# Two expert stages whose late tiles are opened before their last early tiles are done

## The chip, the cores and the metric

The kernel runs on one core of one Trainium2 chip. The metric is the device time of one execution in microseconds (us), the median of several runs. The core has a matrix engine (PE, with its weight loads PEld), a vector engine (DVE), a scalar engine (ACT), a general engine (POOL) and a sync engine (SP) that only issues transfers. Plain loads and stores are issued from SP. Gathers and scatters by an index list are issued from POOL.

## What is computed

The input has 2 sequences of 2048 tokens, 256 wide. Four layers follow, each on the layer-normed stream and added back to it: a state-space layer (Mamba-2), a mixture of experts, an attention layer over the two sequences, and the same mixture of experts again. Only the mixture matters here. It routes every token to 2 of 8 experts:

```python
scores = x @ Wr.T + br                      # 8 scores per token
idx    = top_k(scores + biases, 2)          # two experts for each token
val    = softmax(scores)[idx]; val /= val.sum()
h      = x @ Wl1[e] + bl1[e]                # 256 -> 2*512, for each expert e
y      = (silu(h[:512]) * h[512:]) @ Wl2[e] + bl2[e]      # 512 -> 256
out    = sum over the two experts of val * y
```

All of it is float32.

## The kernel before

**Tiles of tokens by expert.** Class `Experts` (L280) does one mixture; `ffn` (names ending in `_f`) is the first and `last` (names in `_g`) the second. Tokens are handled in 8 groups of 512. When a group is routed (`prepare`, L309), `enter` (L413) scatters an entry for each of its tokens and choices into a table in memory, eight scatters from POOL (L433), sorted by expert. A tile is 256 consecutive entries of one expert (128 for a half tile). For a tile the kernel does this:

- `rows` (L652): SP loads the tile's part of the table, `tab`.
- `load` (L663): SP loads the expert's first weights `w1` (1 MB), second weights `w2` (0.5 MB) and biases `b1`, `b2`.
- `gather` (L680): POOL gathers the tile's tokens from memory into `xs`, 128 at a time.
- `turn` (L702): PE transposes `xs` (4 transposes, L709) into a PSUM bank and ACT copies it out as `xT` (L713).
- `up` (L735): four times `up_part` (L716): PE multiplies `w1` into a bank (`pab`, L722), ACT takes the silu (L730), DVE multiplies into `gT` (L731).
- `down` (L743): PE multiplies `w2` (`pf`, L752), DVE adds the bias part (L765), POOL scatters the rows with addition (L776).

**Early and late tiles.** A tile that is sure to be full can run before all tokens are routed. These are the early tiles: 21 in the first mixture (called f-e0 to f-e20 here), mixed into the state-space layer, and 9 in the second (g-e0 to g-e8), mixed into the attention layer. The profile writes them `_fe` and `_ge`. The others are late tiles (f0, f1, ... and g0, g1, ...): 16 in the first mixture, 28 in the second, and they begin once `plan` (L516) knows every count. A seam is the place where the last early tile gives way to the first late one. Generator `early` (L788) is stepped by the layer around it; what is left of it runs in `tiles.rest()` (L1215 and L1476). Then `run` (L812) takes the late tiles in a loop, three tiles ahead with loads.

**Buffers.** There are two pools. `fe` exists throughout, with two buffers each of `w1`, `w2`, `b2`, `xs`, `y`. `f2` lies in memory that the layer before has given back, and opens with `run` (L817). Early tiles use `fe`; of the late tiles those with an odd place in the sequence use `fe`, those with an even place `f2` (L649). The first late tile has place 21 in the first mixture and 9 in the second, so in both it uses `fe` and its `w1` waits until the last early tile but one has been multiplied.

**Banks.** PSUM banks are handed out by tag, two banks for each of A, B, C and T. An early tile uses only tag B: for its transposes, all four up parts and the down part. A late tile transposes into T and alternates A and B.

**What sets the order.** SP's order is that of the program, by hand (L79). Every engine works its own list in order. Outside `run`, the order on PE, ACT, DVE and POOL comes from a planner that works when the program is built; inside `run` ACT, DVE and POOL stand in the order written (L818) and PE is left to the planner. In `early` a tile is turned, multiplied up and down, and then the next is turned. So in the second mixture SP's list has, one after another, the loads of g-e6, g-e7 and g-e8, then four `tab` loads, then the loads of g0 and g1.

Of the kernel before, what the change touches and what calls it, by code (L numbers as in the profile page):

```python
# [34 lines left out]
NT = NB * L  # L35
# [11 lines left out]
def kernel(  # L47
# [35 lines left out]
    def bank(tag, name):  # L83
        return ps.tile([P, 512], F32, tag=tag, name=name)
# [195 lines left out]
    class Experts:  # L280
        def __init__(self, name, acc, direct=False):
            self.name, self.acc, self.direct = name, acc, direct
            self.seq, self.ts, self.tabs, self.next = [], {}, {}, [0, 0, 0]
            n = NE * NT + TT
            self.table = tc.dram_tile([n + (NE * TT if direct else 0), 3], F32, name=f"table_{name}")
            self.xnd = tc.dram_tile([NT + TT, DM], F32, name=f"xnd_{name}")
            nc.sync.dma_start(self.table[:n, :].rearrange("(p r) c -> p r c", p=P), empty)
            for to in (self.xnd,) if direct else (self.xnd, acc):
                nc.sync.dma_start(to[NT:, :].rearrange("(h p) d -> p h d", p=P), zero)
            self.off = rt2.tile([P, NE], F32, tag=f"off{name}", name=f"off0_{name}")  # L290
            nc.gpsimd.tensor_copy(self.off, region)

            self.pay = const.tile([P, NT // P, 2, 3], F32, name=f"pay_{name}")
            for c, of in ((0, token), (2, place.rearrange("p s b t -> p (s b t)"))):
                nc.gpsimd.tensor_copy(
                    self.pay[:, :, :, c].bitcast(I32), of.unsqueeze(2).to_broadcast([P, NT // P, 2])
                )
            self.rest, self.freed = None, []
            if direct:
                self.rest = const.tile([P, TT // P, 3], F32, name=f"rest_{name}")  # L300
                nc.gpsimd.memset(self.rest, 0.0)
                for c, base in ((0, NT), (2, 0)):
                    nc.gpsimd.iota(
                        self.rest[:, :, c].bitcast(I32), [[P, TT // P]], base=base, channel_multiplier=1
                    )
            self.taken = rt2.tile([P, NE], F32, tag=f"taken{name}", name=f"taken_{name}")
            nc.gpsimd.memset(self.taken, 0.0)
# [208 lines left out]
        def plan(self):  # L516

            name = self.name
            NPT = 2 * NT // TT - len(self.seq)
            NTT = NPT + NHF  # L520
            cnt = rt1.tile([P, NE], F32, tag="cnt", name=f"cnt_{name}")
            nc.vector.tensor_tensor(cnt, self.off, region, ALU.subtract)
# [123 lines left out]

        def tile(self, i, shape, tag, dtype=F32, bufs=2):
            nm, _, _, _, early = self.seq[i]
            pool = fe if early or i % 2 else self.f2  # L649
            return pool.tile(shape, dtype, tag=tag, name=f"{tag}_{nm}", bufs=bufs)  # L650

        def rows(self, i):  # L652
# [38 lines left out]
        def fetch(self, tables, tiles, gather=True):  # L691
            while self.next[0] < min(tables, len(self.seq)):
                self.rows(self.next[0])
                self.next[0] += 1
            while self.next[1] < min(tiles, len(self.seq)):
                self.load(self.next[1])
                self.next[1] += 1
                if gather:
                    for h in range(2):
                        self.gather(self.next[1] - 1, h)  # L700

        def turn(self, i):  # L702
            t = self.ts[i]
            nm, nh = t["nm"], t["nh"]
            n = nh * P
            pt = bank("B" if self.seq[i][4] else "T", f"pxs_{nm}")
            for k in range(KD):
                for h in range(nh):
                    nc.tensor.transpose(  # L709
                        pt[:, k * n + h * P : k * n + (h + 1) * P], t["xs"][:, h, k * P : (k + 1) * P], ident  # L710
                    )
            xT = fe.tile([P, KD * TT], F32, tag="xT", name=f"xT_{nm}")
            nc.scalar.copy(xT[:, : KD * n], pt[:, : KD * n])  # L713
            t["xT"] = xT[:, : KD * n].rearrange("p (k t) -> p k t", k=KD)
# [20 lines left out]
        def up(self, i):  # L735
            t = self.ts[i]
            nm = t["nm"]
            pool = fe if i % 2 else self.f2
            t["gT"] = pool.tile([P, NHT, TT], F32, tag="gT", name=f"gT_{nm}", bufs=1)
            for j in range(NHT):  # L740
                self.up_part(t, j, "AB"[j % 2])
# [46 lines left out]
        def early(self, ready):  # L788

            i = 0  # L790
            while True:
                while i >= len(self.seq):
                    yield
                if not self.seq[i][4]:
                    return
                full = sum(t[4] > 0 for t in self.seq)
                self.fetch(min(i + 2, full), min(i + 2, full))
                self.fetch(full, 0)
                if not i:
                    yield  # L800
                self.turn(i)
                t = self.ts[i]
                t["gT"] = fe.tile([P, NHT, TT], F32, tag="gT", name=f"gT_{t['nm']}", bufs=1)
                for j in range(NHT):
                    self.up_part(t, j, "B")
                    if j % 2:
                        yield
                self.down(i, "B", None)
                i += 1
                yield  # L810

        def run(self):  # L812
            ahead = 3
            first = next(i for i, t in enumerate(self.seq) if not t[4])
            n = len(self.seq)
            with (
                tc.tile_pool(name=f"f2{self.name}", bufs=2) as self.f2,  # L817
                tc.manual_schedule(  # L818
                    engines={mybir.EngineType.Pool, mybir.EngineType.Activation, mybir.EngineType.DVE}
                ),  # L820
            ):
                self.fetch(first + ahead + 1, first + ahead)
                self.turn(first)
                assert self.seq[-1][1] == 2
                for i in range(first, n - 1):
                    self.fetch(i + ahead + 2, i + ahead + 1, gather=False)
                    if i == first + 6:
                        with tc.manual_schedule(engines={mybir.EngineType.PE}):
                            beyond = nc.values_load(self.beyond[0:1, 0:1], min_val=0, max_val=NHF - NIN)
                            self.up(i)  # L830
                    else:
                        self.up(i)
                    self.turn(i + 1)
                    if i > first:
                        self.down(i - 1, "C", i + ahead)
                    else:
                        for h in range(2):
                            self.gather(i + ahead, h)
                    if i == first + 2:
                        yield  # L840
                self.down(n - 2, "C", None)
                self.up(n - 1)
                self.down(n - 1, "C", None)
                with tc.If(beyond > 0):
                    for tile in self.more:
                        i = len(self.seq)
                        self.seq.append(tile)
                        self.fetch(i + 1, i + 1)
                        self.turn(i)
                        self.up(i)  # L850
                        self.down(i, "C", None)

    ffn = Experts("f", tc.dram_tile([NT + TT, DM], F32, name="resid"))
    last = Experts("g", flat(out), direct=True)
# [2 lines left out]
    with tc.tile_pool(name="ssm1", bufs=1) as s1, tc.tile_pool(name="ssm2", bufs=2) as s2:  # L857
# [339 lines left out]
            done = (b, s, t, y)  # L1197
        chunk_out(*done)
        aside.add(routing(*done[:2]))
        while aside.waiting:  # L1200
            aside.step()
            tiles.step()
# [9 lines left out]
    attw = ctx.enter_context(tc.tile_pool(name="attw", bufs=1))  # L1212
    w_qkv_sb = attw.tile([P, KD, 3, AW], F32, name="w_qkv_sb")
    w_o_sb = attw.tile([P, NA, DM], F32, name="w_o_sb")
    tiles.rest()  # L1215
    late = ffn.run()
    next(late)
# [8 lines left out]
    with tc.tile_pool(name="att1", bufs=1) as a1, tc.tile_pool(name="att2", bufs=2) as a2:  # L1226
# [230 lines left out]
        for s in range(NS):  # L1457

            if s + 1 < NS:
                while s + 1 not in inputs:  # L1460
                    aside.step()
                scores(s + 1, range(0, GT // 2))

                aside.waiting.insert(0, entered())
            else:
                aside.rest()
                tiles.step(4)
            mix(s)
            outward(s)
            if s + 1 < NS:  # L1470
                scores(s + 1, range(GT // 2, GT))
                weights(s + 1)
        while aside.waiting:
            aside.step()
            tiles.step()
        tiles.rest()  # L1476

    for _ in last.run():
        pass

# [60 lines left out]
```

## Time and profile before

| | us |
|---|---|
| runs: median, lowest, highest of 3 | 1701.59, 1696.14, 1702.38 |
| profiled execution, its own time | 1703.7 |
| span in that profile (first to last instruction) | 1702.0 |
| PE busy in the span | 1585.8 |
| first seam: last up of an early tile starts, first up of a late one starts | 729.42, 739.84 |
| second seam: the same | 1402.62, 1415.92 |
| late tiles of the second mixture, from there to PE's last matmul | 1415.92 to about 1691.7 |

The time of an execution is 1.7 us more than the span. Lines of the order in time have: start, duration, engine, line, operation, output and inputs, how often, and in brackets the idle time of the engine before it and what ended that. Consecutive instructions of a kind are merged, so a row's duration runs from its first start to its last end. Matmuls overlap a little, so the start of the next row is the better end. In the table of stretches every engine has its busy time and its instruction count, then come the granted clock of PE (1.00 is full), the busy share of the transfer engines and the rate in GB/s.

### The profile page before, as it was taken

The numbers are of one execution on the slowest core, as the hardware profiler recorded it, in microseconds if no ns is written. First come the engines' busy times: TensorE is split into PE (matmuls) and PEld (weight loads), VectorE is DVE, ScalarE is ACT, GpSimd is POOL, SyncE is SP. The second block draws the span as 40 slices with busy tenths as digits, with TensorE's granted clock in tenths as the row PEclk, the third lists the DMA queues.
The fourth block names the chain that finished last, engine by engine and source line by source line (L and its number), as shares of the span: only waits on it lengthen the run. The fifth ranks groups of instructions, "written<-read, shape, count | busy, mean of one in ns | idle before, by whom it ended". The sixth has DMA issues, their size and how long they took to land.

```text
span 1702.0 us, 22149 instructions
## 1 busy us (share of the span) xinstructions
PE 1585.8 (93%) x7088; PEld 1194.0 (70%) x7088; DVE 896.3 (53%) x2471; ACT 674.6 (40%) x1340; POOL 739.0 (43%) x702
## 2 busy tenths in 40 slices
PE   6997988989999989999998999899999979999997
PEld 3665555677767767788984575465768768888886
DVE  6778878837648464422227648447454512222222
ACT  5886867856647543222332202011120322333332
POOL 3356457455545556634441003414140751544443
PEclk9998988999989999999999999999999989999999
DMA  4122211743525455889852312516353686888783
GB/s 157 39 63 49 87 47 41 215 125 89 157 48 176 104 148 134 204 261 315 233 112 78 82 43 62 89 50 138 106 107 104 184 226 179 224 236 225 229 215 51
DMA packets 174744, 231.30 MB, mean 136 GB/s; under 512 B 45920, under 2 KB 138080, under 8 KB 174368
## 3 DMA queue, kind: packets, MB, share of 16 engines
q1 hardware_dynamic: 143520, 193.42, 38.7%
q0 software_dynamic: 31104, 36.42, 11.9%
q8 instruction: 58, 0.95, 0.2%
q14 instruction: 62, 0.51, 0.1%
HBM read 192.72 MB, written 37.06 MB: 135 GB/s over the span
## 4 chain that ended last, share of the span: by engine, by line
PE 46%; DMA 7%; DVE 1%; issue 1%; POOL 1%; SPq 0%; ACT 0%; DVEq 0%; POOLq 0%
PE pab_g L722 9%; PE pao L1430 7%; PE pq L1336 6%; PE pab_f L722 5%; PE pf_g L752 4%; PE pvd L1410 3%; PE pab_ge L722 3%; PE pk L1336 3%; DMA out_dram<-y_g,tab_g 2%; PE pf_f L752 2%; DMA o<-prob 2%; PE pf_ge L752 1%; PE pr_g L330 1%; DMA xs_f<-xnd_f,tab_f 1%; DMA resid<-y_f,tab_f 1%
## 5 line engine op out<-in xcount | busy, mean ns | idle before, releaser
L722 PE MATMUL pab_g<-xT_g,w_g 128*128 128x256 f32 (+1 forms) x896 | 181.4, 361 | 0.0
L722 PE MATMUL pab_fe<-xT_fe,w_fe 128*128 128x256 f32 x672 | 158.3, 390 | 20.7 <-DVE gT_fe L731 17.8
L722 PEld LDWEIGHTS pab_g<-xT_g,w_g 128*128 128x128 f32 x896 | 158.4, 190 | 19.6 <-ACT xT_g L713 0.4
L722 PEld LDWEIGHTS pab_fe<-xT_fe,w_fe 128*128 128x128 f32 x672 | 128.8, 195 | 47.7 <-DVE gT_fe L731 22.3
L776 POOL DMA_INDIRECT out_dram<-y_g,tab_g x51 | 80.3, 1575 | 137.0 <-DVE y_g L765 54.9
L730 ACT ACTIVATE sa_g<-pab_g,b_g 128x256 f32<-128x256 f32 (+1 forms) x112 | 51.0, 455 | 188.0 <-PE pab_g L722 188.0
L731 DVE SCALAR_TENSOR_TENSOR gT_g<-pab_g,b_g,sa_g 128x256 f32<-128x256 f32 (+1 forms) x112 | 51.5, 460 | 128.9 <-ACT sa_g L730 128.9
L1336 PE MATMUL pq<-w_qkv_sb,axT 128*128 128x512 f32 x256 | 117.4, 597 | 0.0
L1006 DVE SCALAR_TENSOR_TENSOR xc<-pre,conv_w_sb,xc 128x512 f32<-128x512 f32 x144 | 113.5, 798 | 5.2 <-ACT xc L998 4.6
L1430 PE MATMUL pao<-w_o_sb,o 128*128 128x256 f32 x512 | 112.3, 380 | 0.0
L1430 PEld LDWEIGHTS pao<-w_o_sb,o 128*128 128x128 f32 x512 | 97.0, 190 | 15.9 <-issue 2.9
L989 PE MATMUL pc<-xT,w_in_sb 128*128 128x512 f32 x192 | 96.3, 631 | 0.4 <-ACT xc L998 0.4
L722 PE MATMUL pab_f<-xT_f,w_f 128*128 128x256 f32 (+1 forms) x512 | 96.4, 346 | 0.0
L433 POOL DMA_INDIRECT table_g<-pay_g,at_g x64 | 62.3, 974 | 71.2 <-DVE w_g L409 39.2
L752 PE MATMUL pf_g<-w_g,gT_g 128*128 128x256 f32 x408 | 92.7, 379 | 0.0
L722 PEld LDWEIGHTS pab_f<-xT_f,w_f 128*128 128x128 f32 x512 | 85.5, 191 | 9.4
L1043 ACT ACTIVATE lt<-lb,cum 128x128 f32<-128x128 f32 x256 | 82.8, 394 | 19.8 <-DMA lb<-sums 19.8
L1336 PEld LDWEIGHTS pq<-w_qkv_sb,axT 128*128 128x128 f32 x256 | 48.4, 191 | 57.9 <-issue 56.2
L776 POOL DMA_INDIRECT resid<-y_fe,tab_fe x42 | 67.0, 1595 | 38.2 <-DVE y_fe L765 22.6
L731 DVE SCALAR_TENSOR_TENSOR gT_fe<-pab_fe,b_fe,sa_fe 128x256 f32<-128x256 f32 x84 | 39.7, 480 | 81.3 <-ACT sa_fe L730 81.2
L1351 ACT ACTIVATE kd<-pk 128x512 f32<-128x512 f32 x32 | 19.1, 597 | 159.1 <-PE pk L1336 90.7
L752 PEld LDWEIGHTS pf_g<-w_g,gT_g 128*128 128x128 f32 x408 | 75.4, 190 | 9.3 <-DVE gT_g L731 0.2
(477 smaller groups left out, 3381.9 us busy)
## 6 DMA issues: line engine op xcount, KB each, us to landing
w_g<-in_wl_dram SPq DMA_DIRECT2D x28, 1024.0 KB, 7.5
w_fe<-in_wl_dram SPq DMA_DIRECT2D x21, 1024.0 KB
lb<-sums SPq DMA_DIRECT2D x32, 512.0 KB, 5.8
w_f<-in_wl_dram SPq DMA_DIRECT2D x16, 1024.0 KB, 6.5
o<-prob SPq DMA_DIRECT2D x32, 512.0 KB, 15.6
w_g<-in_wl_dram SPq DMA_DIRECT2D x28, 512.0 KB, 4.0
w_fe<-in_wl_dram SPq DMA_DIRECT2D x21, 512.0 KB, 6.7
w_ge<-in_wl_dram SPq DMA_DIRECT2D x9, 1024.0 KB, 8.4
```

What stands on the lines that cost most here:

```text
L433: i = nc.gpsimd.indirect_dma_start(out=self.table, out_offset=bass.IndirectOffsetOnAxis(ap=at[:, t, c : c + 1], axis=0), in_=pay[:, t, c, ...
L722: nc.tensor.matmul(p[:, q * n : (q + 1) * n], t["w1"][:, k, c * P : (c + 1) * P], t["xT"][:, k, :], start=(k == 0), stop=(k == KD - 1),)
L730: nc.scalar.activation(sa[:, :n], p[:, 0:n], AF.Silu, bias=t["b1"][:, i : i + 1])
L731: nc.vector.scalar_tensor_tensor(t["gT"][:, i, :n], p[:, n : 2 * n], t["b1"][:, NHT + i : NHT + i + 1], sa[:, :n], ALU.add, ALU.mult)
L752: nc.tensor.matmul(pos[h][:, h * DM : (h + 1) * DM], t["gT"][:, j, h * P : (h + 1) * P], t["w2"][:, j, :], start=(j == 0), stop=(j == NHT ...
L776: j = nc.gpsimd.indirect_dma_start(out=self.acc if self.direct else self.acc[: self.seq[i][4] or NT + TT, :], out_offset=bass.IndirectOffs ...
L989: nc.tensor.matmul(pc, w_in_sb[:, k, DI + c * P : DI + (c + 1) * P], xT[:, k, :], start=(k == 0), stop=(k == KD - 1),)
L1006: nc.vector.scalar_tensor_tensor(xc[:, c, :], pre[:, c, j : j + TG], conv_w_sb[:, c, j : j + 1], xc[:, c, :], ALU.mult, ALU.add,)
L1043: nc.scalar.activation(lt[:, i, :], lb[:, i, :], AF.Relu, bias=g["cum"][:, t, i : i + 1], scale=-1.0)
L1336: nc.tensor.matmul(p, src[:, k, t * P : (t + 1) * P], w_qkv_sb[:, k, j, half * TG : (half + 1) * TG], start=(k == 0), stop=(k == KD - 1),)
L1410: nc.tensor.matmul(pvd, w_qkv_sb[:, k, 2, c * P : (c + 1) * P], xd[:, k, :], start=(k == 0), stop=(k == KD - 1),)
L1430: nc.tensor.matmul(po[:, j * DM : (j + 1) * DM], o[i][:, c, (t + j) * P : (t + j + 1) * P], w_o_sb[:, c, :], start=(c == 0), stop=(c == NA ...
```

## The change

Five edits, all at the two seams.

- **Open.** A new method `open` enters pool `f2` and issues from SP the four `tab` loads and the weights of the late tiles at places first and first + 2, and their gathers. It is called ahead of `tiles.rest()` in both mixtures, so ahead of what is left of `early`. `fetch` skips a tile that is loaded already.
- **Places.** Late tiles now count from the first late tile: it uses `f2`, the second `fe`, the third `f2`.
- **Close.** A flag `close` is set when the layer around has ended its own steps. From then on an early tile's up parts alternate A and B, and its transposes go to T.
- **Turns ahead.** With `close` set, `early` turns the next tile between a tile's up and its down. `early` doesn't turn a tile that has its `xT`.
- **The first late tile.** After the last early tile's up, the next tile is the first late one, which `open` has loaded, so it is turned there; `run` still begins with its own `self.turn(first)`.

```diff
-            pool = fe if early or i % 2 else self.f2
+            pool = fe if early or (i - self.first) % 2 else self.f2
...
             while self.next[1] < min(tiles, len(self.seq)):
-                self.load(self.next[1])
+                i = self.next[1]
                 self.next[1] += 1
-                if gather:
-                    for h in range(2):
-                        self.gather(self.next[1] - 1, h)
+                if i not in self.ts:
+                    self.load(i)
+                    if gather:
+                        for h in range(2):
+                            self.gather(i, h)
...
-            pt = bank("B" if self.seq[i][4] else "T", f"pxs_{nm}")
+            pt = bank("B" if self.seq[i][4] and not self.close else "T", f"pxs_{nm}")
...
-                self.turn(i)
+                if "xT" not in self.ts[i]:
+                    self.turn(i)
...
-                    self.up_part(t, j, "B")
+                    self.up_part(t, j, "AB"[j % 2] if self.close else "B")
                     if j % 2:
                         yield
+
+                if self.close and i + 1 in self.ts:
+                    self.turn(i + 1)
                 self.down(i, "B", None)
...
+        def open(self):
+            self.late = tc.tile_pool(name=f"f2{self.name}", bufs=2)
+            self.f2 = self.late.__enter__()
+            self.fetch(self.first + 4, 0)
+            for i in (self.first, self.first + 2):
+                self.load(i)
+                for h in range(2):
+                    self.gather(i, h)
...
         aside.add(routing(*done[:2]))
+        ffn.close = True
         while aside.waiting:
...
+    ffn.open()
     tiles.rest()
     late = ffn.run()
...
+        last.close = True
         while aside.waiting:
             aside.step()
             tiles.step()
-        tiles.rest()
-
+
+    last.open()
+    tiles.rest()
     for _ in last.run():
```

`self.first` is the number of early tiles, set in `plan`.

More of the change, by code (lines that the diff above doesn't have):

```diff
@@ L283, in __init__ @@
             self.seq, self.ts, self.tabs, self.next = [], {}, {}, [0, 0, 0]
+            self.close = False
             n = NE * NT + TT
@@ L518, in plan @@
             name = self.name
-            NPT = 2 * NT // TT - len(self.seq)
+            self.first = len(self.seq)
+            NPT = 2 * NT // TT - self.first
             NTT = NPT + NHF
@@ L737, in up @@
             nm = t["nm"]
-            pool = fe if i % 2 else self.f2
+            pool = fe if (i - self.first) % 2 else self.f2
             t["gT"] = pool.tile([P, NHT, TT], F32, tag="gT", name=f"gT_{nm}", bufs=1)
@@ L810, in early @@
                 yield
+        def open(self):
[6 more added lines that the diff above has]
+                    self.gather(i, h)
         def run(self):
             ahead = 3
-            first = next(i for i, t in enumerate(self.seq) if not t[4])
+            first = self.first
             n = len(self.seq)
             with (
-                tc.tile_pool(name=f"f2{self.name}", bufs=2) as self.f2,
                 tc.manual_schedule(
@@ L851, in run @@
                         self.down(i, "C", None)
+            self.late.__exit__(None, None, None)
     ffn = Experts("f", tc.dram_tile([NT + TT, DM], F32, name="resid"))
```

## The prediction

> **What bounds the kernel now.** I read the page first, then the waits of PE around each seam, then PE, SP and POOL in order of time there. PE is busy for 93% of the span:
>
> ```profile
> PE 1585.8 (93%) x7088; PEld 1194.0 (70%) x7088; DVE 896.3 (53%) x2471; ACT 674.6 (40%) x1340; POOL 739.0 (43%) x702
> ```
>
> So only time in which PE waits can be won. At the second seam (waits of PE from 1300 to 1416 us: total, times, longest):
>
> ```profile
> PE pxs_g L709 <- DMA xs_g<-xnd_g,tab_g: 7.8, 3, 3.3
> PE pab_ge L722 <- ACT xT_ge L713: 3.0, 4, 1.0
> PE pab_ge L722 <- DVE gT_ge L731: 1.7, 2, 1.2
> ```
>
> PE in order of time shows where:
>
> ```profile
> 1381.61 7.17 PE L722 MATMUL pab_ge<-xT_ge,w_ge 128*128 128x256 f32 x32 [0.68 <-ACT xT_ge L713]
> 1388.62 3.67 PE L752 MATMUL pf_ge<-w_ge,gT_ge 128*128 128x256 f32 x16
> 1392.13 0.60 PE L709 MATMUL pxs_ge<-ident,xs_ge 128*128 128x128 f32 x4
> 1396.05 1.33 PE L709 MATMUL pxs_g<-ident,xs_g 128*128 128x128 f32 x4 [3.33 <-DMA xs_g<-xnd_g,tab_g]
> ...
> 1402.62 9.95 PE L722 MATMUL pab_ge<-xT_ge,w_ge 128*128 128x256 f32 x32
> 1412.41 3.67 PE L752 MATMUL pf_ge<-w_ge,gT_ge 128*128 128x256 f32 x16
> 1415.92 7.07 PE L722 MATMUL pab_g<-xT_g,w_g 128*128 128x256 f32 x32
> ```
>
> The transposes of g0 and half of g1 stand ahead of g-e8's up. PE waits for their gathers with work at hand, 1392.7 to 1402.6. Then the up takes 9.95 us, not 7.07. The stretches (clock is the third number from the end) say why:
>
> ```profile
> 1392.00:1394.00 2.00, 0.73 (x6) 0.42 (x4) 0.88 (x2) 0.59 (x1) 1.56 (x2) 1.00 1.12 333
> 1404.00:1406.00 2.00, 2.00 (x6) 1.59 (x5) 0.00 (x0) 0.00 (x0) 0.03 (x1) 0.50 0.79 243
> 1412.00:1414.00 2.00, 2.00 (x11) 1.63 (x10) 0.48 (x1) 0.47 (x1) 0.00 (x0) 1.00 0.28 25
> ```
>
> At the first seam only 1.47 us goes to a gather:
>
> ```profile
> 728.73 0.85 PE L709 MATMUL pxs_f<-ident,xs_f 128*128 128x128 f32 x5 [1.47 <-DMA xs_f<-xnd_f,tab_f]
> ```
>
> **The change, part by part.** A tile's undisturbed work on PE, start to start, is turn 0.44, up 7.0, down 3.5.
>
> *Turns ahead and banks A/B.* Each turn followed by its up costs 0.68 us of waiting for ACT's copy; with the down between, nothing, as 3.5 us of matmuls cover 0.6 us of copy. At the second seam the built list of the changed kernel has on PE, from group 7's `pk_g` matmuls (done at 1313.4) on: g-e2's turn, g-e1's down, g-e2's up, g-e3's turn, g-e2's down, g-e3's up with group 8's transposes and scores inside it (0.9 and 1.7), then in the same way turn, down, up to g-e6's up, g-e7's turn, g-e6's down, g-e8's turn, g0's turn twice, g-e7's up and down, g-e8's, g0's up. Added up with the durations above, g-e3's up ends at 1337.8, and g-e4's at 1349.7 (before: 1353.2): gone are the DVE waits (1.25, 0.47) and the 0.68s, while g-e4's up waits about 1 us, because ACT has an exponential between two table loads (1.28 each) ahead of its copy. g-e6's up then ends at 1371.6, its down at 1375.5. The move of group 8 has a price off PE: its `pk_g` comes at 1339.0 in place of 1335.65. By the same adding on DVE (3.5 us to its payload, held by two `y_ge`) and on POOL (eight scatters at 1.27, two additions at 1.9 among them) its last table scatter starts at 1358.2, not 1354.63.
>
> *Open, SP's queue.* In the changed list the four `tab` loads and eight loads of g0 and g2 stand ahead of g-e7's and g-e8's weights, which before went out at 1365.22 and 1377.02. These rows of SP price the step:
>
> ```profile
> 1377.02 0.38 SPq L668 DMA_DIRECT2D w_ge<-in_wl_dram  x1
> ...
> 1383.29 3.87 SPq L656 DMA_DIRECT2D tab_g<-table_g  x4
> 1388.81 0.37 SPq L668 DMA_DIRECT2D w_g<-in_wl_dram  x1
> ```
>
> The tabs wait for the last table scatter: 1358.2 plus 4.6 to 5.6 us of landing (the scatters' least and median there) is 1363.2. Four tabs take 3.9, so g0's and g2's eight loads go from 1367.8 to 1372.5. g-e7's `w1` then waits for more: in the built list it reuses the completion counter of g0's `w1`, so it goes out when that has landed, 1367.8 + 7.9 = 1375.7. Ahead of it in the transfer engines are 2 x 1.63 MB, with itself 4.26 MB, and beside it three gathers and a scatter, about 1 MB. At the 300 to 340 GB/s of the busy stretches (314 at 727 to 740, 323 at 1392 to 1403) 5.3 MB take 16 to 18 us: landed at 1384 to 1386; I take 1384.5, as the transfers beside it need not all be done first. Bounds: 1379.5 if the gathers cost nothing and 370 GB/s holds; 1388 if they have the lower rate of 250.
>
> *Open, POOL's queue.* POOL now has g0's and g2's gathers, four, ahead of g-e8's two. They wait for the tabs to land (3.7 us): g0 from 1366.9, g2 from 1369.5, g-e8 from 1372.1, the last issued at 1373.4. Gathers of these stages landed in 5.2 us (median from 1365 to 1390) to 8.1 us (the chain that ended last, 1394.17 to 1402.3); among the weights I take 7: 1380.4. On PE g-e8's turn, then g0's, then g0's again stand ahead of g-e7's up. So PE idles from 1375.5 to 1380.4, does 1.3 to 2.6 us of transposes, and starts g-e7's up at 1384.5. Queued behind this on POOL: g-e5's additions, which nothing needs before g-e7's down.
>
> *The clock.* A row speaks against this part: between 900 and 904.3 PE idled 4.3 us and the clock was 0.82 at 902 to 904, 0.50 until 910:
>
> ```profile
> 902.00:904.00 2.00, 0.00 (x0) 0.00 (x0) 1.39 (x7) 0.00 (x0) 1.68 (x1) 0.82 1.05 351
> 904.00:906.00 2.00, 1.71 (x6) 1.18 (x7) 1.32 (x7) 0.11 (x1) 1.23 (x1) 0.50 1.06 359
> 908.00:910.00 2.00, 2.00 (x5) 0.86 (x5) 2.00 (x9) 0.78 (x1) 0.00 (x0) 0.50 0.03 10
> ```
>
> The Trainium skill, "TensorE: Matmul & The Clock Gate", part 1, says that the clock halves after one idle window of about 3.4 us, that the windows run free of the program, and that one busy window restores it. By the row, a gap of 4.9 us halves the clock and about 5 us of work costs 2.5 more. By the rule it is a matter of phase, as a 4.9 us gap need not hold a whole window: 0 or up to 3.4. I take 2.5.
>
> *Sum of the second seam.* 1384.5 + 21.0 (g-e7 and g-e8, up and down) + 2.5 = 1408.0 for g0's up, against 1415.92: **7.9 us less**. From g0 on PE had no gap in the profile until 1691, so the lead is kept.
>
> *First seam.* The loads already stood ahead of `open`, so SP's list hardly moves. Won: three 0.68s, the 1.47, DVE waits of 1.2. Lost: 0.44 for turning f0 twice, and f-e17 and f-e18 are both turned before f-e17's up, so it waits for f-e18's gather. That was issued last at 686.39; now by my walk at 687.2, landing 5.5 later at 692.7, so the up starts at 693.2, not 692.44. From there 44.4 us to f0's up: 737.6 against 739.84, **2.2 us less**. The transfer engines are nearly full after it (0.95 from 740 to 800, and PE waits 3.7 us for gathers at 781 to 792), which can take this back or, with the tile at first + 2 loaded early, shrink that wait: 0 to 4.
>
> *Nothing.* Places move buffers only. The second copy of `xT` is on ACT under g-e8's down, 3.5 against 0.6.
>
> **Sum.** 7.9 + 2.2 = 10.1: a span of 1691.9 for 1702.0, and with the 1.7 around it 1693.6 for the profiled 1703.7. That execution lies 2.1 above the median of the runs, so from the median 1701.59: **1691.5**.
>
> **The rivals.** *The stall moves whole.* The wait for gathers at g-e8 becomes one for gathers and weights at g-e7, with the slow clock: g-e7's up at 1388, clock 3.4, g0's up at 1412.4, 3.5 less, with 0 to 2 of the first seam 1698 to 1696.5. For it: the later bound of the landing above, and that the same megabytes move in the same saturated queue. Against: before, g0's gather was issued at 1390.31; now 23 us earlier.
>
> *No stall is left.* Gathers land in 5.2 us and weights by 1379 to 1381, the clock stays up: g0's up at about 1400, 16 less, with 2.2 more 1683.5. For it: before, g-e7's `w1` had 16 us to land and needed 8. Against: 4.26 MB at 370 GB/s is 11.5 us from 1367.8, already 1379.3.
>
> *Slower.* One mechanism: in SP's queue g-e7's weights stand behind `tab` loads that depend on all routing. If the last scatter lands later, the weights do, microsecond for microsecond, and all PE's work stands behind them. Even with the first seam's 2.2, break-even is g-e7's up at 1394.6 (1418.1 - 21.0 - 2.5), 10.1 later than I take; 0.5% slower is 18.6 later, so a last scatter at 1377. The skill's "DMA: Bandwidth & Descriptors", on issuing engines that are not separate queues, says that transfers of SP and POOL run on the same 16 engines and interleave. By the row, a table scatter landed in 4.6 us at best and 9.6 at worst in that stretch; by the rule, g-e6's weights and gathers push it to the worst, 4 us more. With a seam that goes wrong elsewhere I'd write 1711.
>
> **How the numbers follow.** Part of the stall stays (1685 to 1697, likeliest 1691.5): 0.55. Moves whole (1697): 0.20. No stall (1683.5): 0.13. Slower (1711): 0.12. About 0.5%, 8.5 us, is what a measurement can tell here: below 1693.1 is faster. Of the first case three quarters lie there, with the third case 0.54. Same: 0.20 and a quarter of the first, 0.34. Slower: 0.12. The range of 8 in 10 takes in the case without stall and that of the moved stall with its spread: 1683 to 1700.
>
> **What would show it.** Right: no 0.68 gaps before `pab_ge` in the last five early tiles; idle time before `pxs_ge` of g-e8 of some 5 us (gather) and a shorter one before g-e7's `pab_ge`; g-e8's `pab_ge` at 7.1; 51 gathers of `xs_g` still, but one `pxs_g` group of four more. At the first seam f0's `pxs_f` without a wait. Wrong: a wait of PE on g-e7's `w_ge` past 1390, `tab_g` issued after 1366, or the gap between f-e17's turn and up above 3 us.

## The result, and the profile after

The changed kernel took 1706.38 us, the median of 22 runs, beside 1697.8 for 22 runs of the kernel before on the same chip: a ratio of 1.0043 (95% interval 1.0028 to 1.0057). Predicted were 1691.5, in a range of 1683 to 1700. The gain of 10 us did not come, and a little was lost.

The span of the profiled execution doesn't show the loss: it is 1700.5, and that of before was 1702.0. But this execution ran 7.4 us ahead of before at 650 us, before the first edit acts, and only 1.6 ahead where the second seam begins (group 7's `pk_g` at 1311.41 against 1313.05). From the last `po` of the state-space layer, where the first seam begins, to the end it takes 1041.8 us, and before took 1035.8. So each stretch has to be read for itself. PE's busy share is what it was (the page, busy time by engine):

```profile
PE 1584.6 (93%) x7096; PEld 1196.5 (70%) x7096; DVE 895.9 (53%) x2471; ACT 675.1 (40%) x1342; POOL 734.3 (43%) x702
```

The waits of PE at the second seam, 1300 to 1416 us (in total, times, longest):

```profile
PE pab_ge L726 <- DMA w_ge<-in_wl_dram: 8.0, 2, 4.3
PE pxs_ge L713 <- DMA xs_ge<-xnd_g,tab_ge: 3.5, 2, 3.2
```

All three kinds of wait of before are gone: 12.5 us for g0's gather, ACT's copies and DVE. In their place PE waits 11.5 us for loads, 8.0 of them for weights. PE in order of time:

```profile
1336.58 1.46 PE L756 MATMUL pf_ge<-w_ge,gT_ge 128*128 128x256 f32 x6
...
1342.12 1.19 PE L726 MATMUL pab_ge<-xT_ge,w_ge 128*128 128x256 f32 x2 [3.71 <-DMA w_ge<-in_wl_dram]
1343.10 4.47 PE L756 MATMUL pf_ge<-w_ge,gT_ge 128*128 128x256 f32 x10
1347.37 7.09 PE L726 MATMUL pab_ge<-xT_ge,w_ge 128*128 128x256 f32 x30
...
1376.37 3.62 PE L756 MATMUL pf_ge<-w_ge,gT_ge 128*128 128x256 f32 x16
1383.20 0.45 PE L713 MATMUL pxs_ge<-ident,xs_ge 128*128 128x128 f32 x1 [3.22 <-DMA xs_ge<-xnd_g,tab_ge]
...
1390.94 9.68 PE L726 MATMUL pab_ge<-xT_ge,w_ge 128*128 128x256 f32 x32 [4.29 <-DMA w_ge<-in_wl_dram]
...
1414.39 7.07 PE L726 MATMUL pab_g<-xT_g,w_g 128*128 128x256 f32 x32
```

In the middle of g-e3's down (6 of its 16 matmuls are done) stands the first part of g-e4's up, and it waits 3.7 us for g-e4's `w1`. Then the ten other matmuls take 4.3 us to the next row, where 2.2 is normal: the clock is at half. Then g-e8's gather is waited for at 1383.2, and g-e7's `w1` at 1390.94, again with the clock at half after it: 9.5 us to the next row for g-e7's up, not 6.9. g0's up stands at 1414.39; predicted were 1408.0, before it was 1415.92. Counted from that `pk_g`, it takes 102.98 us where before took 102.87. Nothing is won at this seam.

The clock in the stretches after the two weight waits (third number from the end):

```profile
1344.00:1346.00 2.00, 2.00 (x6) 1.64 (x5) 0.00 (x0) 0.00 (x0) 1.39 (x3) 0.50 1.09 329
...
1392.00:1394.00 2.00, 2.00 (x6) 1.64 (x5) 0.00 (x0) 0.00 (x0) 1.48 (x2) 0.50 1.02 403
```

At the first seam f0's `pxs_f` has no wait any more and the 0.68s are gone, but before f-e17's up PE waits 3.5 us for f-e18's gather (0.73 and then 2.81), and the up after it runs partly at half clock:

```profile
686.37 0.90 PE L713 MATMUL pxs_fe<-ident,xs_fe 128*128 128x128 f32 x3 [2.81 <-DMA xs_fe<-xnd_f,tab_fe]
687.06 8.28 PE L726 MATMUL pab_fe<-xT_fe,w_fe 128*128 128x256 f32 x32
...
732.36 7.17 PE L726 MATMUL pab_f<-xT_f,w_f 128*128 128x256 f32 x32 [0.24 <-ACT xT_f L717]
```

From the layer's last `po` at this seam to f0's up it takes 73.64 us (before 73.70), and to the first matmul after the late tiles 224.82 (before 224.02).

So at the two seams and in the late tiles between them less than 1 us is lost. The rest of the 6 us lies between the seams, in the attention layer, which no edit touches. From the first matmul after the late tiles to group 7's `pk_g` it takes 427.9 us, before took 422.9, with the same instructions in the same order on PE, DVE, ACT and POOL. More than half of it arises at one place, where PE waits for DVE, and DVE for a load of the attention layer (`o<-prob`). PE and DVE before, then in the changed kernel:

```profile
1265.97 5.54 PE L722 MATMUL pab_ge<-xT_ge,w_ge 128*128 128x256 f32 x24 [2.15 <-DVE y_ge L765]
...
1264.44 0.69 DVE L1418 TENSOR_TENSOR o<-pvd,o 128x512 f32<-128x512 f32 x1 [6.21 <-DMA o<-prob]
```

```profile
1262.73 7.13 PE L726 MATMUL pab_ge<-xT_ge,w_ge 128*128 128x256 f32 x24 [3.63 <-DVE y_ge L769]
...
1261.20 0.69 DVE L1438 TENSOR_TENSOR o<-pvd,o 128x512 f32<-128x512 f32 x1 [7.68 <-DMA o<-prob]
```

After the longer wait the clock is at half for 3.4 us; after the shorter one it stays up.

### The profile page after: what moved, and what is told of

Its sections match the earlier page's. It is cut to its first block, busy times and chain, and to the rows that moved or that the text cites. A ratio compares the mean times of both kernels' runs of the same rounds, so it can differ in the third digit from the quotient of the medians.

```text
span 1700.5 us, 22158 instructions
## 1 busy us (share of the span) xinstructions
PE 1584.6 (93%) x7096; PEld 1196.5 (70%) x7096; DVE 895.9 (53%) x2471; ACT 675.1 (40%) x1342; POOL 734.3 (43%) x702
## 4 chain that ended last, share of the span: by engine, by line
PE 62%; DMA 13%; DVE 12%; POOL 6%; issue 3%; ACT 3%; SPq 1%; DVEq 0%; POOLq 0%; ACTq 0%
PE pab_g L726 9%; PE pao L1450 7%; PE pab_fe L726 5%; PE pab_f L726 5%; PE pq L1356 5%; PE pf_g L756 4%; PE pf_fe L756 3%; DVE xc L1024 3%; DMA lb<-sums 3%; PE pvd L1430 2%; PE pk L1356 2%; PE pab_ge L726 2%; DMA o<-prob 2%; PE pi L1120 2%; PE pf_f L756 2%
## 5 line engine op out<-in xcount | busy, mean ns | idle before, releaser
L726 PE MATMUL pab_fe<-xT_fe,w_fe 128*128 128x256 f32 x672 | 157.4, 389 | 17.1 <-DVE gT_fe L735 16.8
L726 PE MATMUL pab_ge<-xT_ge,w_ge 128*128 128x256 f32 x288 | 70.4, 402 | 11.6 <-DMA w_ge<-in_wl_dram 8.0
L780 POOL DMA_INDIRECT resid<-y_fe,tab_fe x42 | 67.0, 1596 | 32.4 <-DVE y_fe L769 12.5
```

The lines of the kernel that those rows point to most:

```text
L726: nc.tensor.matmul(p[:, q * n : (q + 1) * n], t["w1"][:, k, c * P : (c + 1) * P], t["xT"][:, k, :], start=(k == 0), stop=(k == KD - 1),)
L780: j = nc.gpsimd.indirect_dma_start(out=self.acc if self.direct else self.acc[: self.seq[i][4] or NT + TT, :], out_offset=bass.IndirectOffs ...
```

## The experiments

**How they are read.** "New waits" was the theory from this profile: each seam has traded its old waits for waits on other loads, which halve the clock. Every kernel was timed against the kernel before on its own chip, a different one for each set, and the sets differ. In three of the four sets before takes 1718 to 1723 us, in the last 1698.8, as in the first measurement. Each run has its mean granted clock, so its time can be split: time x clock is what it would take at full clock, time x (1 - clock) what the half clock takes away, if PE worked all through. The table has the differences to before in the means of the runs, and in brackets before's own two parts. Each of these differences is uncertain by 1 to 3.5 us (95%). And the right column is not a price by itself, since PE also waits at half clock: in the first profile of before it works in 78 of 104 us at half clock. Among before's own runs, time rises by 1.0 us for each us of half clock in the fourth set, but by 0.6 to 0.7 in the other three.

| kernel | ratio (95% interval) | at full clock, us | half clock, us |
|---|---|---|---|
| *first set* | | (1666.3) | (51.6) |
| first seam alone | 1.0005 (0.9991 to 1.0020) | -1.9 | +2.9 |
| second seam alone | 0.9990 (0.9977 to 1.0003) | -3.2 | +1.8 |
| turns and banks alone | 0.9977 (0.9961 to 0.9992) | -6.9 | +2.6 |
| opening alone | 1.0036 (1.0017 to 1.0055) | +3.4 | +3.4 |
| *second set* | | (1666.5) | (52.1) |
| before, again | 0.9992 (0.9976 to 1.0008) | -0.1 | -1.5 |
| changed kernel | 0.9999 (0.9982 to 1.0016) | -4.7 | +3.5 |
| one tile opened | 0.9964 (0.9951 to 0.9978) | -7.9 | +1.6 |
| turns and banks, second seam | 0.9969 (0.9952 to 0.9986) | -5.4 | -0.9 |
| *third set* | | (1670.1) | (53.6) |
| PE's order by hand | 1.0011 (0.9998 to 1.0023) | -2.3 | +4.2 |
| gather early, weights not | 0.9968 (0.9957 to 0.9980) | -9.3 | +2.8 |
| one tile opened, second seam | 0.9950 (0.9931 to 0.9969) | -7.0 | -1.3 |
| changed kernel | 1.0003 (0.9990 to 1.0016) | -5.3 | +6.6 |
| *fourth set* | | (1653.2) | (45.8) |
| changed kernel | 1.0030 (1.0011 to 1.0049) | -1.5 | +7.4 |
| gather early, second seam | 0.9968 (0.9950 to 0.9985) | -5.7 | 0.0 |
| one tile opened, second seam | 1.0006 (0.9983 to 1.0029) | -2.5 | +3.8 |

**One seam at a time.** For the first seam alone, and in the same way with `ffn` for the second (the other seam has its places by parity and its opening of `f2` as before):

```diff
-        last.close = True
...
-    last.open()
     tiles.rest()
```

> The change at the first seam alone; the second seam as before. Theory 'new waits' (each seam trades its old wait for waits on other loads, and the halved clock after them takes the rest): PE waits 2 to 3.5 us for f-e18's gather before f-e17's up, wins that back by f0's up, whole time 0 to 3 us above before. Rival 'second seam alone' (the whole loss comes from g-e7's weights behind the tabs): 2 us below before, as the prediction has it for this seam.

> The change at the second seam alone; the first as before. 'New waits': 2 to 5 us above before, with waits of PE of about 3.7 us on g-e4's w1, 3 us on g-e8's gather and 4 us on g-e7's w1, and g0's up no earlier than 2 us before where it was. 'Second seam alone': the whole loss, 7 us or more above before. If neither seam costs anything and the loss is chance of the clock elsewhere: within 2 us of before.

Neither moves the time: 0.05% more and 0.10% less, inside their intervals. The second seam alone as the seat of the whole loss is out, and a win of 2 us at the first seam isn't seen either. In both the means have less work and more half clock, each by about its uncertainty.

**One half of the edits at a time.** First without the two `open()` calls, then with them but without the two `close` lines.

```diff
-    ffn.open()
...
-    last.open()
```

> Banks A/B and turns ahead at both seams, nothing opened early. 'New waits': in the built list g0's turn now stands after g-e8's down, so the gather that cost before 7.8 us has 10 us more; g-e7's and g-e8's weights stand ahead of the tabs again; so at the second seam only the wait on g-e4's w1 (3.7 us) is left, g0's up 10 us earlier than before, and the whole time 5 to 10 us below before. Rival 'banks' (alternating banks and the second turn disturb ACT and DVE and cost by themselves): 3 us or more above before.

> Tabs and loads of the first and third late tile opened early at both seams, early tiles on bank B in the old order. 'New waits': in the built list g0's turn stands ahead of g-e6's up, so PE waits 4 to 6 us for g0's gather there and again for g-e7's w1, which is issued after eight loads; g0's up 0 to 6 us later than before; whole time 2 to 8 us above before. Rival 'banks' (the loss is from the alternating banks): 3 us or more below before.

Turns and banks alone are 0.23% faster, opening alone is 0.36% slower. So the half that was to bring the large gain is the one that costs, and "banks" is out. The size for turns and banks (4.2 us) is below the 5 to 10 expected. Its profile still has waits of 3.1 us for `gT` before g-e8's down and of 2.0 at g-e5's.

**The chip.** The profiles of that set all have a wait of PE of up to 9 us near 700 us, with the change at the first seam and without it.

> The kernel before, unchanged, as one more entry: a second profile of it, from the chip of these runs, and its granted clock. Every theory: no difference (within 0.15%). Open before it runs: whether the stall of some 8 us near 700 us, which the runs of the first set show at the first seam with and without the change, belongs to the chip (then it is here too) or to the edits (then it isn't).

It does not belong to the edits: the kernel before has it too. ACT in order of time, kernel before on the second set's chip:

```profile
696.54 0.58 ACT L713 COPY xT_fe<-pxs_fe 128x512 f32<-128x512 f32 x1 [12.40 <-remote]
```

ACT's copy starts 12.4 us after its last work, and "remote" says that what ended the wait is nothing that the trace names. Waits of 3 to 13 us with this ending are in every profile of the first three sets, on ACT or DVE, and in none of the first measurement and the fourth set. What they wait for stays open, and so does whether it is the chip or what else ran on it at the time.

> The changed kernel as it is, beside the variants. If the two seams add up as in the single-seam runs (+0.05% and -0.10%): within 3 us of before. If the loss of 7 us comes again: the single seams do not add up, or the chip matters. 'New waits': PE waits at g-e4's w1 (3 to 4 us), g-e8's gather (3) and g-e7's w1 (4), the clock at half after them.

Level with before, while the work is 4.7 us less. Its waits at the second seam are 3.1 us for g-e7's `w1` and none for g-e4's, where the first profile had 8.0 for both: on this chip PE is held elsewhere (4.1 us for `gT` in g-e5's down), and the loads catch up meanwhile.

**What stands ahead of g-e7's weights.**

```diff
-            for i in (self.first, self.first + 2):
+            for i in (self.first,):
```

> As the changed kernel, but each seam opens only its first late tile early, not the third. 'New waits', with g-e7's w1 delayed by what stands ahead of it in SP's queue: four loads fewer are ahead (2.9 us of issue, 1.6 MB), and in the built list g0's turn now comes after g-e8's up, so the waits at g-e7 shrink from 7.5 to 3 us or less, g0's up 5 to 8 us earlier than in the changed kernel, whole time 4 to 8 us less than the changed kernel. If the tabs alone (waiting for the last table scatter) hold g-e7's weights: no more than 3 us less.

0.36% less than before and 0.35% less than the changed kernel on this chip, as "loads ahead" had it. But two things differ: with fewer loads the planner also puts g0's transposes after g-e8's up. So PE's order alone was changed, in the kernel with both tiles opened:

```diff
     last.open()
-    tiles.rest()
+    with tc.manual_schedule(engines={mybir.EngineType.PE}):
+        tiles.rest()
```

> The changed kernel with PE's order at the second seam kept as written: g-e8's and g0's transposes no longer stand ahead of g-e7's up (they come after g-e7's and g-e8's up, as in the kernel that opens one tile); SP's list and POOL's unchanged, so both tiles' loads are still ahead of g-e7's. Theory 'loads' (g-e7's w1 is late because of what stands before it in SP's queue): PE still waits 3 us or more at g-e7's up, and the time is within 2 us of the changed kernel. Theory 'order' (the transposes ahead of g-e7's up did it): 4 us or more below the changed kernel, as with one tile.

The order is not it. PE's waits in this run, from 1380 us to g0's up:

```profile
PE pab_ge L726 <- DMA w_ge<-in_wl_dram: 6.7, 1, 6.7
```

With g-e8's and g0's transposes out of the way, one single wait of 6.7 us for g-e7's `w1` is left, and the time is 0.11% above before. The loads decide. The opposite end, no weights early at all:

```diff
             for i in (self.first, self.first + 2):
-                self.load(i)
...
+            i = self.first
+            xs, ids = self.tile(i, [P, 2, DM], "xs"), self.tabs[i].bitcast(I32)
...
+                nc.gpsimd.indirect_dma_start(
```

The cut leaves out the rest of the gather. The weights of the first late tile are loaded in `run`.

> As the changed kernel at both seams, but early there go only the tabs and the first late tile's gather; its weights come after g-e8's. 'Loads': g-e7's w1 waits only for the tabs, so PE waits there 2 us or less, and the time is 4 to 8 us below before, about as with one tile opened early. If the tabs alone, which wait for the last table scatter, were enough to make g-e7's w1 late: a wait of 3 us or more there and no more than 3 us below before.

No wait for weights at the second seam in its profile; 0.32% less than before and 0.35% less than the changed kernel on this chip, with the largest cut of work of all (9.3 us). The changed kernel with and without the early weights is thus the plainest pair: the weights (and the third tile's gather, which goes with them) cost what the rest wins.

**The second seam alone, with one tile.**

> Banks A/B and turns ahead at the second seam alone, nothing opened early anywhere. 'New waits': PE's list has g0's turn after g-e8's down and no load is late, so g0's up 8 to 10 us earlier than before and the whole time 5 to 10 us less than before, at least as good as with both seams (4.2 less). Rival 'banks': no gain at this seam, within 3 us of before.

> One late tile opened early, turns ahead and banks A/B, at the second seam alone; the first seam as before. The single-seam runs gave 1 us more for the first seam and the one-tile kernel 6 us less for both, so 6 to 8 us below before, the best of all; if the first seam gains as the prediction said (2.2), 4 us below.

Turns and banks at the second seam alone win 0.31%, at the small end of what was expected. With one tile opened it is 0.50% less, the best ratio, but from six runs.

**The first measurement again.**

> The changed kernel again. The first measurement had it 0.43% above before (0.28 to 0.57), the second 0.01% below (-0.18 to +0.16). If the difference belongs to the chip, one of the two comes back here according to how far before's own time lies from 1698 or 1718 us; if it is chance of the runs, something between.

> The changed kernel once more. Two sets have it level with before (-0.01% and +0.03%), the first measurement 0.43% above. If the first was chance or one chip's: again within 0.2% of before. If not: 0.3 to 0.6% above. In either case the split found in the two sets: the time at full clock (time times mean granted clock) 4 to 6 us below before, what the half clock takes 3 to 7 us above.

Level with before where before takes 1723 us, and 0.30% slower where it takes 1699. So the first measurement was no chance: without the unnamed waits the change costs 0.3 to 0.4%, and with them nothing. In the last set the work is 1.5 us less and the half clock 7.4 more. The changed kernel had 53.2 us of half clock in the 22 runs of the first measurement, the same as here.

Three of the profiles without unnamed waits show where this comes from: the first of before, the first of the changed kernel, and its profile in the last set. In each cell is the length of the stretch, and in brackets how long the clock is at half in it (us):

| stretch | before | changed | changed, last set |
|---|---|---|---|
| first seam, to f0's up | 73.7 (0) | 73.6 (3.4) | 70.7 (0) |
| late tiles of the first mixture | 150.3 (0) | 151.2 (3.4) | 149.5 (0) |
| attention layer, to `pk_g` | 422.9 (13.7) | 427.9 (17.1) | 429.7 (23.9) |
| second seam, to g0's up | 102.9 (13.7) | 103.0 (20.5) | 103.9 (20.5) |
| late tiles of the second mixture, to the end | 286.1 (8.9) | 286.1 (9.5) | 286.1 (9.6) |

The second seam has 6.8 us more at half clock than before. But most of the time lost stands in the attention layer, at the wait for `o<-prob` shown above, which is 3.73 us in the last set. The two kernels that follow, run in the same set, have that wait too (2.89 and 3.06 us, each followed by half clock). Only one profile of before exists without unnamed waits, so whether the edits lengthen this wait, or that one profile was lucky there, stays open.

> One late tile opened early at the second seam alone, again, as the first time had six undisturbed runs only. Expected 0.35 to 0.6% below before.

> Second seam alone: turns ahead, banks A/B, tabs and g0's gather early, g0's weights after g-e8's. If weights that are opened early cost nothing once the third tile's are gone: as the kernel with one tile opened at this seam (0.50% below before), within 0.15% of it. If even one tile's loads hold g-e7's: 2 us or more better.

The expected gain of one tile at the second seam was missed: 0.06% above before on this chip. Its profile has both waits for weights again; PE in order of time:

```profile
1346.64 1.19 PE L726 MATMUL pab_ge<-xT_ge,w_ge 128*128 128x256 f32 x2 [4.27 <-DMA w_ge<-in_wl_dram]
...
1388.46 10.09 PE L726 MATMUL pab_ge<-xT_ge,w_ge 128*128 128x256 f32 x32 [5.34 <-DMA w_ge<-in_wl_dram]
```

With one tile's 1.5 MB of weights ahead of it, g-e7's `w1` is still waited for 5.3 us, and the clock is at half after it. With the gather early and no weights, 0.32% is won (5.5 us in the medians). SP and then PE of that kernel, in order of time:

```profile
1366.85 3.86 SPq L659 DMA_DIRECT2D tab_g<-table_g  x4
1371.55 0.37 SPq L671 DMA_DIRECT2D w_ge<-in_wl_dram  x1
...
1381.69 0.38 SPq L671 DMA_DIRECT2D w_g<-in_wl_dram  x1
```

```profile
1379.03 7.07 PE L727 MATMUL pab_ge<-xT_ge,w_ge 128*128 128x256 f32 x32
...
1401.53 7.17 PE L727 MATMUL pab_g<-xT_g,w_g 128*128 128x256 f32 x32 [0.24 <-ACT xT_g L718]
```

g-e7's `w1` goes out at 1371.55, right behind the tabs, and PE starts g-e7's up at 1379.03 without a wait; g0's weights follow at 1381.69 and are there in time. From group 7's `pk_g` to g0's up it takes 89.9 us, 13 less than in the profile of before; the medians of the runs differ by less than half of that. This kernel beats both; with both seams opened so, it did on the other kind of chip (0.9968). What it still waits for at this seam is g-e4's `w1`, 4.1 us. Its tabs go out as late as the changed kernel's (1366.85 and 1366.56), so late tabs do little harm where no megabytes stand between them and g-e7's `w1`.

## Why the prediction was wrong

**What held.** Up to g-e3's up the walk was right: its end was put at 1337.8, and 1336.14 is that less the lead of 1.64. No 0.68 is left before `pab_ge` of the last five early tiles. Three steps held for themselves: the clock's price after the wait at g-e7 (2.5, measured 2.6), the stalls' places at g-e8's transposes and g-e7's up, and the tabs as what holds SP. At the first seam f-e17's up (693.2) came at 692.74 in the fourth set's profile, whose time up to there is level with before's, and f0's up (737.6) at 736.83. The gain at the first seam is there when the clock stays up (70.7 us for 73.70); in the first profile, where the same wait halved it, it is gone (73.64), and the runs of the first seam alone do not show it.

**The step that failed: "g-e4's up waits about 1 us, because ACT has an exponential between two table loads".** It waited 3.71 us, and for its weights. The prediction moved PE's work ahead at the second seam and asked of each step what ACT and DVE owe it, but not when its load lands. g-e4's `w1` stands in SP's list behind group 8's stores, the first of which waits 14 us for an addition by POOL to land, before as after. SP before, then in the changed kernel:

```profile
1334.58 0.45 SPq L318 DMA_DIRECT2D xnd_g<-xn_g  x1
1336.48 0.38 SPq L668 DMA_DIRECT2D w_ge<-in_wl_dram  x1
```

```profile
1332.64 0.45 SPq L319 DMA_DIRECT2D xnd_g<-xn_g  x1
1334.58 0.38 SPq L670 DMA_DIRECT2D w_ge<-in_wl_dram  x1
```

So it moved by 1.9 us, about the lead of 1.64, and landed after 7.5. Before, PE needed it at 1346.24. Now PE was there at 1338.41: the 0.68s and DVE's waits are gone, and the list has two of g-e4's matmuls inside g-e3's down, ahead of the last ten of it, where the prediction read turn, down, up. As an estimate from these rows, with the ten (2.2 us) first PE would have waited 1.5 us. More than half of the lateness of g-e7's up comes from this. DVE in order of time, and POOL:

```profile
1347.62 0.88 DVE L769 SCALAR_TENSOR_TENSOR y_ge<-pf_ge,tab_ge,by_ge 128x256 f32<-128x256 f32 x2 [5.93 <-PE pf_ge L756]
1348.41 0.18 DVE L411 TENSOR_REDUCE pay_g<-w_g 128x4 f32<-128x32 f32 x1
```

```profile
1352.27 1.80 POOL L780 DMA_INDIRECT out_dram<-y_ge,tab_ge  x1 [0.30 <-DVE half_g L585]
1354.38 1.12 POOL L434 DMA_INDIRECT table_g<-pay_g,at_g  x1 [0.30 <-DVE gT_ge L735]
...
1360.94 0.95 POOL L434 DMA_INDIRECT table_g<-pay_g,at_g  x1 [0.31 <-issue]
```

The last part of group 8's payload stands on DVE behind `y_ge` of g-e3, which waits 5.9 us for g-e3's down, in which the matmul for g-e4 is stuck. POOL idles 3.4 us for it, with six table scatters still to come. The last of them starts at 1360.94, not 1358.2. SP after that:

```profile
1366.56 4.00 SPq L658 DMA_DIRECT2D tab_g<-table_g  x4
1371.34 0.37 SPq L670 DMA_DIRECT2D w_g<-in_wl_dram  x1
...
1377.30 0.38 SPq L670 DMA_DIRECT2D w_ge<-in_wl_dram  x1
```

The tabs go at 1366.56 (predicted: 1363.2), the first loads at 1371.34 (1367.8), and g-e7's `w1` at 1377.30 (1375.7). The prediction counted from before's times and this execution runs 1.64 ahead of them, so by its own count the loads are 5.2 us late, not 3.5. Tabs after 1366 were its own sign of being wrong.

**The second term: the landing of g-e7's `w1`.** 16.7 us were taken from the first late load's issue to it, for 5.3 MB; it took 19.6. The rate was right: 281 and 339 GB/s in the two parts make 6.3 MB, 321 GB/s over all. The bytes were 1 MB too few. The likely reason is that transfers issued after it share the engines (g-e7's `w2`, g-e8's weights, g1's gathers); which bytes they were isn't shown. By the prediction's count g-e7's up is 8.1 us late: 5.2 are the later start and 2.9 this. Together they are about the 7.9 us that the seam was to win. Where the upper bound of 1388 was drawn, only the rate was varied, and 5.3 MB at 250 GB/s would have made 1389. These two terms explain why nothing was won at this seam. That the weights ahead of g-e7's are what costs, the runs show: without them the kernel is 0.32% faster than before, both with the two seams changed and with the second alone, although g-e4's wait is still there in the profile of the latter. No run took away g-e4's wait alone, so its share rests on the traces.

**The clock.** The prediction charged the half clock at one place, 2.5 us, and asked whether a gap of 4.9 us would trip it. It did not ask the same for a gap of 3.7, since it had none. At the second seam the clock was at half for 20.5 us, in 14.5 of which PE works, not the 5 that it charged. The runs have 7.4 us more of half clock than before, where before takes 1699; of this the profiles put a part at the seams and a part in the attention layer, as the table of stretches has it.

**Where it started from.** The median of three runs, 1701.59, lay 3.8 above that of 22. The profiled execution of before had 52.2 us of half clock, and the mean of 51 runs of the fourth set is 45.8. This surplus lies ahead of the seams, where it was at half clock for 68 us and the other four profiles without unnamed waits for 48 to 61. Whether its stall at g0's gather is what an ordinary execution has, no run shows. The second profile of before (with unnamed waits) has 1.4 us there and no half clock behind it, though PE was held 3.6 us before.

**What stays open.** The two terms account for the missing 8 us. They do not account for the loss. The medians are 8.6 us apart, the two profiles 6.0 from the first seam on, and 5.0 of these lie in the attention layer.

**The rivals.** "The stall moves whole" (1697) was nearest in mechanism: a wait for gathers and weights at g-e7 and the slow clock. It had g-e7's up at 1388, measured 1390.94. "Slower" named tabs ahead of g-e7's weights, but needed the last scatter at 1377. It came at 1361. The time rose all the same, by less than the 0.5%, through things that no case held: g-e4's weights, the 1 MB more, and a wait and the clock in the attention layer.

## What to carry to other kernels

When a change lets an engine reach its work sooner, list for every moved step the load that it needs, its issue and its landing; a load that the change doesn't move becomes the next wait. Many waits of 0.7 us are cheaper on PE than their sum in one wait, because here the long one was always followed by half clock and the short ones almost never: fetch early what is small (here rows of 256 KB a tile) and leave the megabytes that are needed later behind those that are needed first. Split the runs' time by their mean clock before a gain or a loss is put down to a cause. Compare profiles stretch by stretch, also where nothing was edited, and don't take one profile's worst stall for the usual one.

## What the runs showed of the hardware

**Waits of PE from 1 us up can halve the clock.** In the 17 profiles of this case, between 100 and 1680 us, these are the gaps of PE that stand alone (less than 0.5 us of other idle time in the 6.9 us before and the 3.5 after). Counted is how many were followed by half clock, within 3.5 us of their end:

| gap, us | gaps | followed by half clock |
|---|---|---|
| 0.4 to 1 | 161 | 2 |
| 1 to 2 | 151 | 19 |
| 2 to 3 | 77 | 38 |
| 3 to 3.5 | 8 | 7 |
| 3.5 and more | 71 | 71 |

So in these profiles a wait of 3.7 us was never a matter of phase. The low stretches last 3.4, 6.8, 10.2 or 13.7 us. The Trainium skill, "TensorE: Matmul & The Clock Gate", part 1, gives one idle window of about 3.4 us as the condition. The window's length agrees with the low stretches. But by that condition gaps of 2 to 3 us would cost nothing, and here half of them were followed by at least 3.4 us at half clock, which is 1.7 us of work if PE is busy all through (an estimate from these figures).

**The same program on other chips.** Before takes 1698 to 1699 us on two occasions and 1718 to 1723 on three others, with ACT and DVE in waits of 3 to 13 us that the trace can't name. A change that is 0.3 to 0.4% slower on the first kind was level on two of the others. Each of the four sets ran on one chip, so chip and occasion can't be told apart.
